# Attention with residual norms on one core: a third y tile, longer norm waits, and another split of the softmax sums

## The chip, the cores and the metric

The kernel runs on one core of one Trainium2 chip. Its five instruction streams are TensorE (PE; its weight loads, which overlap the matmuls, are shown as PEld), VectorE (DVE), ScalarE (ACT), GpSimd (POOL) and SyncE (SP), which here only issues DMAs. The metric is device time in microseconds (us), lower is better.

## What is computed

The input is x with 8 frames of 2048 rows and 256 channels, and an adjacency matrix of 2048 x 2048 that masks the attention. Cut to what matters:

```
qkv = x @ w_qkv ; split into q, k, v of 8 heads x 32
scores = q @ k.T / sqrt(32), -1e9 where adj == 0
t = softmax(scores) @ v
u = layernorm(x + t) * ln1_g + ln1_b
h = relu(u @ w1 + b1)
w = layernorm(u + h @ w2 + b2) * ln2_g + ln2_b
out = layernorm(x + w)
```

Each output row thus goes through three layer norms. Everything is in fp32.

## The kernel before

**Blocks.** The rows of a frame are cut into four chunks of 512 query rows (`qc`), the heads into two halves of four heads (`g`), the keys into 16 blocks of 128 rows (`mb`). One item is `(f, qc, g, mb)`: 128 keys against 512 queries for four heads. There are 8 x 4 x 2 x 16 = 1024 items, 128 to a frame, 32 to a chunk, 16 to a group `(f, qc, g)`. The scores are kept with the keys on the partitions, so no softmax needs a transposition, and no maximum is subtracted.

**One pass of the loop** (lines 599 to 629) is called pass t here, counted within the frame where a number below 129 is given. It issues, in this order: mask loads and new side work, then `advance(t)` (side work that is due), the exponential of item t+1 (ACT, L237, in place on one p tile of 128 x 2048), the scores of item t+2 (eight PE matmuls, L230, then two mask additions on DVE, L233, from PSUM into a new p tile), the product with V of item t (eight matmuls, L249, into one PSUM bank over the 16 blocks), and `add_up` of item t. There are 12 p tiles.

**The sums under the softmax.** The 16 exponentials of a group have to be added over the keys. That is split three ways. `POOLED` blocks are added on POOL into the tile of block 0 (L271). Blocks of a chain in `MOVED` are added by a DMA that accumulates in memory (issued by POOL, L268) into the tile of the chain's first block; each such DMA must find the one before it in its chain landed. `ALONE` is not added. `denominator` then lets TensorE sum what is left, four tiles, with a matrix of ones (L315): eight matmuls a tile into one PSUM bank. It copies the result with ACT (L317), transposes it and takes reciprocals. In the very last group the blocks from 11 on are not added beforehand, and TensorE takes eight tiles.

**Side work** is written as generators, kept in the list `fill`, sorted by a due time. Each pass gives a credit of 2200 PE cycles (`STEP`), which does not add up over passes:

```python
state["credit"] = min(max(state["credit"], 0) + STEP, KEPT)
return finish or state["credit"] >= UNIT or min(due) <= t
```

A unit of eight matmuls of 512 columns costs 2048, four transposes 1400. So a pass carries one unit or four transposes, and more than that only when something is past its due time. A generator's `yield n` sleeps n passes; `BANK` asks for the one spare PSUM bank, `MORE` keeps it for the next unit (its generator is then the holder, and nobody else gets the bank), `WAIT` keeps it while nothing may be issued yet. `TURNED` waits for the buffer of the feed-forward, `ROOM` for the number of tails in flight, `INPUTS` for a slot among three input tiles.

**A chunk's end.** Two passes after a group's last item (time `t`) its `denominator` starts, due at t + 8. When the second half's is done, `outcome` (L333) asks for `ROOM`, takes a `y` tile (two of them), transposes and scales the attention result (`divide`, DVE L353) and lets POOL issue a DMA that adds x to it (L339). `begin` is the chunk's last item + 6. At begin + 10, due at begin + 26, `tail` starts: `norm` (statistics on DVE, L278 and L279, one row of tiles per pass; four small operations on POOL, L283 to L287; two passes later four activations on ACT, L290), `feed_forward` (transposes, then POOL's L459 and L461, then w1 and w2 matmuls at L54, and DVE's L483), a second `norm`, POOL's L363 and L365, a DMA that adds x (L367), seven passes of sleep, a third `norm`, and the output's DMA on SP (L370). For the chunk before the very last, `per=2` takes two rows of tiles per pass, starting at begin + 5 with due at begin + 8. The very last chunk has its own `finish`, cut into two halves of rows that are issued alternately.

**Projections.** `NEXT` (L546) says at which pass of a frame work for the next frame begins: `turn` transposes x, `ask` computes queries, `project(c, g)` a K tile and a V tile. These come from pools of 11 buffers each (L71, L73). A K or V tile of this frame's chunk c and half 0 is last read at pass 96 + 4c + 3.

**Queues.** ACT, DVE, POOL and SP each work strictly in the order of issue. So an addition on POOL, the four small operations of a norm, the g and b rows of a tail and the issue of accumulating DMAs all stand in one line, and so do the exponentials and the activations of a norm on ACT. SP's line holds the loads of x and masks and the output.

Of the kernel before, what the change touches and what calls it, by code (L numbers as in the profile page):

```python
# [61 lines left out]
def fast_path(ctx, tc, cst, x, adj, out, RS):  # L62
# [5 lines left out]
    dp = ctx.enter_context(tc.tile_pool(name="dp", bufs=1, space=bass.MemoryType.DRAM))  # L68
    mkp = ctx.enter_context(tc.tile_pool(name="mkp", bufs=MB // 2 + 1))
    ld = ctx.enter_context(tc.tile_pool(name="ld", bufs=LD))  # L70
    kp = ctx.enter_context(tc.tile_pool(name="kp", bufs=3 * NCK - 1))  # L71
    qp = ctx.enter_context(tc.tile_pool(name="qp", bufs=4))
    vp = ctx.enter_context(tc.tile_pool(name="vp", bufs=3 * NCK - 1))  # L73
    pp = ctx.enter_context(tc.tile_pool(name="pp", bufs=12))
    work = ctx.enter_context(tc.tile_pool(name="work", bufs=1))
    yp = ctx.enter_context(tc.tile_pool(name="yp", bufs=2))
    op = ctx.enter_context(tc.tile_pool(name="op", bufs=1))
    small = ctx.enter_context(tc.tile_pool(name="small", bufs=4))

# [174 lines left out]

    POOLED = (0, 3, 6, 8, 11, 13, 15)
    MOVED = ((1, 4, 7, 10), (2, 5, 9, 12))
    ALONE = 14

    ENDED = MB - 5
    SUM = 4
# [11 lines left out]
    def norm(t, per=1):  # L274
        mv = small.tile([P, TPC, nc.vector.BN_AGGR_DIM], F32, name="mv")
        for j in range(TPC):
            st = small.tile([P, nc.vector.BN_STATS_DIM], F32, name="st")
            nc.vector.bn_stats(st, t[:, j, :])  # L278
            nc.vector.bn_aggr(mv[:, j, :], st)  # L279
            if j % per == per - 1:  # L280
                yield 1
        rs = small.tile([P, TPC], F32, name="rs")
        nc.gpsimd.tensor_scalar(rs, mv[:, :, 1], EPS, 1.0, op0=ALU.add, op1=ALU.mult)  # L283
        nc.gpsimd.tensor_tensor(rs, rs, cst["mhalf"], ALU.pow)  # L284
        nb = small.tile([P, TPC], F32, name="nb")
        nc.gpsimd.tensor_tensor(nb, mv[:, :, 0], rs, ALU.mult)
        nc.gpsimd.tensor_scalar(nb, nb, -1.0, 1.0, op0=ALU.mult, op1=ALU.mult)  # L287
        yield 2
        for j in range(TPC):
            nc.scalar.activation(t[:, j, :], t[:, j, :], AF.Identity, bias=nb[:, j:j + 1], scale=rs[:, j:j + 1])  # L290
            if j % per == per - 1:
                yield 1
# [3 lines left out]

    def denominator(f, qc, g, ready):
        grp = (f, qc, g)
        blocks = [ALONE] + [chain[0] for chain in MOVED + (POOLED,)]
        late = {len(blocks) - 1: ready}  # L300
        if (f, qc, g) == items[-1][:3]:
            blocks = [POOLED[0], 11, 12, MOVED[1][0], 13, 14, MOVED[0][0], 15]
            late = {n: len(items) - k for n, k in ((2, 2), (3, 1), (4, 1), (5, 0), (6, 0), (7, 0))}
        yield BANK
        ps = bank()
        for n, block in enumerate(blocks):
            if n:
                yield MORE
            while state["now"] < late.get(n, 0):
                yield WAIT  # L310
            term = PT.pop((f, qc, g, block))
            state["credit"] -= 4 * CH
            for h in range(4):
                r = D * h
                nc.tensor.matmul(ps[r:r + D, :], cst["ones"], term[:, h, :], start=(n == 0), stop=(n == len(blocks) - 1))  # L315
        dT = op.tile([P, CH], F32, name="dT")
        nc.scalar.copy(dT, ps)  # L317
        yield 1
        yield BANK
        ps = bank()  # L320
        transposes(ps, [dT[:, j::TPC] for j in range(TPC)])
        if g == 0:
            RC[f, qc] = op.tile([P, TPC, H], F32, name="rc")
        rc = RC[f, qc]
        den = ps.rearrange("p (j c) -> p j c", c=P)[:, :, ::D]
        nc.vector.reciprocal(rc[:, :, 4 * g:4 * g + 4], den)
        nc.vector.tensor_tensor(RS[:, 0], RS[:, 0], den, ALU.add)
        nc.vector.tensor_tensor(RS[:, 1], RS[:, 1], den, ALU.min)
        if g == 1:
            begin = items.index((f, qc, g, LAST)) + SUM + 2  # L330
            start(begin, outcome(f, qc) if (f, qc) != (F - 1, NCK - 1) else finish(f, qc), begin)

    def outcome(f, qc):  # L333
        yield ROOM
        state["tails"] += 1
        xin = x[f, qc * CH:(qc + 1) * CH, :].rearrange("(p j) c -> p j c", p=P)
        y = yp.tile([P, TPC, C], F32, name="y")
        yield from divide(f, qc, y)
        nc.gpsimd.dma_start(y, xin, accum_op=ALU.add)  # L339
        begin = items.index((f, qc, 1, LAST)) + SUM + 2  # L340
        if (f, qc) == (F - 1, NCK - 2):
            start(begin + 5, tail(f, qc, y, xin, 2), begin + 8)
        else:
            start(begin + 10, tail(f, qc, y, xin), begin + 26)

    def divide(f, qc, y):
        rc = RC.pop((f, qc))
# [9 lines left out]
    def tail(f, qc, y, xin, per=1):  # L357
        yield from norm(y, per)
        yield from feed_forward(y)
        yield 1  # L360
        z = y
        yield from norm(z, per)
        nc.gpsimd.tensor_tensor(z, z, rows(cst["g2r"]), ALU.mult)  # L363
        yield 1
        nc.gpsimd.tensor_tensor(z, z, rows(cst["be2r"]), ALU.add)  # L365
        yield 1
        nc.gpsimd.dma_start(z, xin, accum_op=ALU.add)  # L367
        yield 7
        yield from norm(z, per)
        nc.sync.dma_start(out[f, qc * CH:(qc + 1) * CH, :].rearrange("(p j) c -> p j c", p=P), z)  # L370
        state["tails"] -= 1
# [65 lines left out]
    def finish(f, qc):  # L437
        y = yp.tile([P, TPC, C], F32, name="y")
        xr, xb = state["rows"]
        yield from divide(f, qc, y)  # L440
        yT, hT = (work.tile([P, 2, CH], F32, name=n) for n in ("turned", "hT"))
        dst = out[f, qc * CH:(qc + 1) * CH, :].rearrange("(p j) c -> p j c", p=P)
        both = [half_rows(h, y, xr, xb, yT, hT, dst) for h in range(2)]
        while both:
            for e in list(both):
                if next(e, both) is both:
                    both.remove(e)

    def feed_forward(y):
        yield TURNED  # L450
# [18 lines left out]
                columns(ps, w1s[:, a, d * P:(d + 1) * P], yT[:, a, :], start=(a == 0), stop=(a == 1))  # L469
            nc.scalar.activation(hT[:, d, :], ps, AF.Relu, bias=cst["b1s"][:, d:d + 1], scale=1.0)  # L470
        state["turned"] = False
        yield 1
        z = y
        for jj in range(0, TPC, 2):
            yield BANK
# [28 lines left out]
    def advance(t, finish=False):  # L504
# [15 lines left out]
        for e in list(fill):  # L520
            while e[2] is not None and e[0] <= t and e is not state["holder"]:
# [4 lines left out]
                elif e[2] < INPUTS:  # L526
                    inputs = inputs and not any(u is not None for u in live[:INPUTS - e[2]])
                    if not inputs:
                        break
                elif e[2] == TURNED and state["turned"] or e[2] == ROOM and state["tails"] == 2:  # L530
                    break
                resume(e, t)
            while e is state["holder"] and more():
# [7 lines left out]
    def ask(f, c):  # L541
# [2 lines left out]
        give(xT)  # L544

    NEXT = {1: [(turn, 0)], 2: [(ask, 1)], 20: [(turn, 1)], 34: [(ask, 2)], 40: [(project, 0, 0)], 50: [(turn, 2)],  # L546
            60: [(project, 1, 0)], 66: [(ask, 3)], 72: [(turn, 3)], 80: [(project, 2, 0)], 98: [(ask, 0)], 100: [(project, 3, 0)],
            104: [(project, 0, 1)], 108: [(project, 1, 1)], 112: [(project, 2, 1)], 116: [(project, 3, 1)]}

    def begin():  # L550
        todo = deque((qc, c) for qc in range(NCK) for c in range(NCK))
# [319 lines left out]
```

## Time and profile before

| what | us |
|---|---|
| time, median of 3 runs (lowest to highest) | 3245.36 (3242.5 to 3246.28) |
| the profiled execution's own time | 3246.02 |
| its span, first to last instruction | 3244.1 |
| PE busy, 28996 matmuls | 3109.4 (96%) |
| DVE busy | 2735.7 (84%) |
| POOL busy | 2592.2 (80%) |
| ACT busy | 2435.8 (75%) |
| L271, sums on POOL, 381 times | 4.793 each |
| L268, issue of an accumulating DMA on POOL, 383 times | 0.956 each |
| L233, mask addition on DVE, 2048 times | 1.218 each |
| L363, L365, L459, L461 on POOL, 31 times each | 2.663, 2.687, 2.552, 2.679 each |
| L339, L367, issue of the DMAs that add x, 31 times each | 0.960, 1.071 each |
| L283, L284, L286, L287 on POOL, 93 times each | 0.194, 1.036, 0.201, 0.195 each |
| mean granted TensorE clock | 0.985 of full speed |

The profile is of one execution. A line of the timeline gives start, duration, engine, line of the kernel, operation, what is written from what, and in brackets the idle time of the engine before it with what ended it; "issue" there is a time in which the profile shows nothing that was waited for. The chain of waits is followed back from the last instruction: each piece is what the next one waited for. Matmuls are pipelined and their ends are modelled, so that a busy PE is not always a PE at its peak. Times are counted from the span's start.

### The profile page before, as it was taken

Reading aid. Unit: us, or ns where it says so; the run is one execution under the profiler, and the core shown is the slowest. Engines: PE = TensorE matmul, PEld = TensorE weight load, DVE = VectorE, ACT = ScalarE, POOL = GpSimd, SP = SyncE. Lnnn points to the kernel's source line nnn. Section 1 sums busy time; section 2 is a strip of 40 time slices with the busy share of each in tenths; the row PEclk is TensorE's granted clock in tenths of the full one; section 3 lists DMA queues with packets and bytes.
Section 4 is the critical chain, followed back from the end, with each engine's and each line's share of the span. In section 5 each row is a group of like instructions: output and inputs, shape, how many; then the busy total and the mean of one; then the engine's idle time right before and its main releaser. Section 6 shows DMA issues by size and latency. Waiting matters only on the chain.

```text
span 3244.1 us, 68406 instructions
## 1 busy us (share of the span) xinstructions
PE 3109.4 (96%) x28996; PEld 979.0 (30%) x28996; DVE 2735.7 (84%) x3203; ACT 2435.8 (75%) x1941; POOL 2592.2 (80%) x1358
## 2 busy tenths in 40 slices
PE   7899999999999999999999999999999999998985
PEld 4222333223332233322233323323233323332222
DVE  4888888888888888888988888888888888888975
ACT  3667778777777777778777778777778777777774
POOL 0568888888878888788887888888888788878884
PEclk8899999999999999999999999999999999999998
DMA  9688779778879788788787879878788878877763
GB/s 320 145 181 185 183 176 199 178 177 196 181 176 207 171 188 193 159 195 200 178 181 174 185 174 221 177 167 198 173 192 197 177 168 198 181 171 161 166 145 86
DMA packets 153240, 590.52 MB, mean 182 GB/s; under 512 B 15040, under 2 KB 67776, under 8 KB 103904
## 3 DMA queue, kind: packets, MB, share of 16 engines
q0 software_dynamic: 64416, 434.80, 66.9%
q1 hardware_dynamic: 87696, 149.98, 13.1%
q8 instruction: 229, 3.75, 0.4%
q10 hardware_dynamic: 816, 1.31, 0.1%
q14 instruction: 83, 0.68, 0.1%
HBM read 146.67 MB, written 37.75 MB: 57 GB/s over the span
## 4 chain that ended last, share of the span: by engine, by line
PE 75%; DVE 7%; POOL 5%; issue 4%; DMA 4%; ACT 2%; DVEq 0%; POOLq 0%; ACTq 0%
PE s L230 27%; PE x L249 24%; PE x L54 14%; PE x L315 6%; DVE p L233 6%; PE x L95 4%; DMA p<-p 3%; POOL p L271 2%; ACT p L237 1%; DMA mask<-md 1%; POOL y L365 1%; DVE st L278 1%; POOL y L363 0%; POOL y L461 0%; POOL y L459 0%
## 5 line engine op out<-in xcount | busy, mean ns | idle before, releaser
L233 DVE TENSOR_TENSOR p<-s,mask 128x1024 f32<-128x1024 f32 x2048 | 2409.3, 1218 | 372.7 <-PE s L230 209.9
L237 ACT ACTIVATE p<-p 128x2048 f32<-128x2048 f32 x1024 | 1956.1, 1910 | 521.4 <-DVE p L233 465.6
L271 POOL TENSOR_TENSOR p<-p 128x2048 f32<-128x2048 f32 x381 | 1825.5, 4793 | 223.7 <-ACT p L237 221.3
L230 PE MATMUL s<-qT,kT 32*128 32x512 f32 x8192 | 1173.8, 643 | 40.8 <-DVE p L233 35.9
L249 PE MATMUL x<-p,v 128*32 128x512 f32 x8192 | 1096.0, 607 | 16.7 <-ACT p L237 16.4
L268 POOL DMA_DIRECT2D p<-p x383 | 359.3, 956 | 306.9 <-ACT p L237 88.3
L230 PEld LDWEIGHTS s<-qT,kT 32*128 32x128 f32 x8192 | 321.1, 183 | 644.7 <-DVE p L233 587.2
L249 PEld LDWEIGHTS x<-p,v 128*32 128x32 f32 x8192 | 161.6, 108 | 797.8 <-issue 310.6
L315 PE MATMUL x<-p,ones 128*32 128x512 f32 x2080 | 268.2, 594 | 17.9 <-POOL p L271 11.1
L290 ACT ACTIVATE y<-y,nb,rs 128x256 f32<-128x256 f32 x372 | 218.7, 590 | 40.4 <-POOL nb L287 40.4
L54 PE MATMUL x<-in,wqkv 128*32 128x512 f32 x1888 | 243.5, 592 | 0.0
L278 DVE BATCH_NORM_STATS2 st<-y 128x6 f32<-128x256 f32 x372 | 154.9, 416 | 5.1 <-DMA y<-in_x_dram 5.1
L54 PE MATMUL x<-turned,w1s 128*32 128x512 f32 x992 | 123.5, 596 | 0.4 <-ACT in L166 0.4
L54 PE MATMUL x<-w2s,hT 128*32 128x256 f32 x2016 | 121.8, 382 | 2.1 <-DVE y L483 2.1
L54 PEld LDWEIGHTS x<-wqkv,in 128*32 128x32 f32 x3584 | 102.2, 110 | 63.4 <-issue 58.9
L315 PEld LDWEIGHTS x<-p,ones 128*32 128x32 f32 x2080 | 66.3, 110 | 178.2 <-issue 140.4
L54 PE MATMUL x<-wqkv,in 128*32 128x128 f32 x3584 | 117.3, 273 | 0.0
L54 PEld LDWEIGHTS x<-in,wqkv 128*32 128x32 f32 x1888 | 61.7, 110 | 140.9 <-issue 113.7
L284 POOL TENSOR_TENSOR rs<-rs,mhalf 128x4 f32<-128x4 f32 x93 | 96.3, 1036 | 7.8
L54 PEld LDWEIGHTS x<-w2s,hT 128*32 128x32 f32 x2016 | 65.4, 111 | 75.0 <-issue 33.0
L363 POOL TENSOR_TENSOR y<-y,g2r 128x1024 f32<-128x1024 f32 x31 | 82.5, 2663 | 5.3 <-ACT y L290 5.3
L461 POOL TENSOR_TENSOR y<-y,be1b2r 128x1024 f32<-128x1024 f32 x31 | 83.0, 2679 | 0.6
(116 smaller groups left out, 1335.7 us busy)
## 6 DMA issues: line engine op xcount, KB each, us to landing
p<-p POOLq DMA_DIRECT2D x383, 1024.0 KB, 10.4
in<-xd SPq DMA_DIRECT2D x87, 512.0 KB, 10.6
mask<-md SPq DMA_DIRECT2D x248, 128.0 KB, 7.9
y<-in_x_dram POOLq DMA_DIRECT2D x62, 512.0 KB, 8.1
p<-in_adj_dram SPq DMA_DIRECT2D x16, 1024.0 KB, 10.7
out_dram<-y SPq DMA_DIRECT2D x31, 512.0 KB, 6.2
in<-in_x_dram SPq DMA_DIRECT2D x29, 512.0 KB, 15.5
xd<-in SPq DMA_DIRECT2D x28, 512.0 KB, 11.2
```

The lines of the kernel that those rows point to most:

```text
L54: nc.tensor.matmul(out[r:r + D], lhsT[:, r:r + D], rhs, start=start, stop=stop)
L95: nc.tensor.transpose(ps[:, j * P:(j + 1) * P], s, ident)
L230: nc.tensor.matmul(ps2[half][:, j, :], KT[f, mb // TPC, g][r:r + D, (mb % TPC) * P:(mb % TPC + 1) * P], QT[f, qc, g][r:r + D, :], start=Tr ...
L233: nc.vector.tensor_tensor(pt[:, 2 * half:2 * half + 2, :], ps, MK[f, qc, mb // 2][:, mb % 2, None, :].to_broadcast([P, 2, CH]), ALU.add)
L237: nc.scalar.activation(PT[item], PT[item], AF.Exp, scale=1.0 / math.sqrt(D))
L249: nc.tensor.matmul(O[grp][r:r + D, :], V[f, mb // TPC, g][:, mb % TPC, r:r + D], PT[item][:, h, :], start=(mb == 0), stop=(mb == LAST))
L268: nc.gpsimd.dma_start(PT[f, qc, g, chain[0]], PT.pop(item), accum_op=ALU.add)
L271: nc.gpsimd.tensor_tensor(first, first, PT.pop(item), ALU.add)
L278: nc.vector.bn_stats(st, t[:, j, :])
L284: nc.gpsimd.tensor_tensor(rs, rs, cst["mhalf"], ALU.pow)
L290: nc.scalar.activation(t[:, j, :], t[:, j, :], AF.Identity, bias=nb[:, j:j + 1], scale=rs[:, j:j + 1])
L315: nc.tensor.matmul(ps[r:r + D, :], cst["ones"], term[:, h, :], start=(n == 0), stop=(n == len(blocks) - 1))
```

## The change

The change takes one buffer from each of the pools of K and V tiles and gives one to the pool of y tiles; `ROOM` then admits three tails. The blocks are split anew among POOL (now 0, 3, 6, 8, 10, 12, 14), the DMA chains (1, 4, 7, 11 and 2, 5, 9, 13) and TensorE alone (15), and the four tiles reach TensorE in another order. The sleeps of a tail are longer: four passes instead of two between a norm's POOL part and its ACT part (three where per=2), three instead of one before w2, nine instead of seven before the third norm (eight where per=2). A tail starts at begin + 11, due at begin + 28. In the last frame all tails take two rows per pass and start at begin + 9, due at begin + 12. `finish` sleeps one pass after each round of its two halves. Some projections begin later in the frame, as their buffers come free later.

```diff
-    kp = ctx.enter_context(tc.tile_pool(name="kp", bufs=3 * NCK - 1))
+    kp = ctx.enter_context(tc.tile_pool(name="kp", bufs=3 * NCK - 2))
-    vp = ctx.enter_context(tc.tile_pool(name="vp", bufs=3 * NCK - 1))
+    vp = ctx.enter_context(tc.tile_pool(name="vp", bufs=3 * NCK - 2))
-    yp = ctx.enter_context(tc.tile_pool(name="yp", bufs=2))
+    yp = ctx.enter_context(tc.tile_pool(name="yp", bufs=3))
...
-    POOLED = (0, 3, 6, 8, 11, 13, 15)
-    MOVED = ((1, 4, 7, 10), (2, 5, 9, 12))
-    ALONE = 14
+    POOLED = (0, 3, 6, 8, 10, 12, 14)
+    MOVED = ((1, 4, 7, 11), (2, 5, 9, 13))
+    ALONE = 15
...
@@ norm
-        yield 2
+        yield max(5 - per, 2)
@@ denominator
-        blocks = [ALONE] + [chain[0] for chain in MOVED + (POOLED,)]
-        late = {len(blocks) - 1: ready}
+        blocks = [ALONE, MOVED[0][0], POOLED[0], MOVED[1][0]]
+        late = {2: ready - 1, 3: ready}
         if (f, qc, g) == items[-1][:3]:
-            blocks = [POOLED[0], 11, 12, MOVED[1][0], 13, 14, MOVED[0][0], 15]
+            blocks = [POOLED[0], 11, 12, MOVED[0][0], 13, 14, MOVED[1][0], 15]
@@ outcome
-        if (f, qc) == (F - 1, NCK - 2):
-            start(begin + 5, tail(f, qc, y, xin, 2), begin + 8)
+        if f == F - 1:
+            start(begin + 9, tail(f, qc, y, xin, 2), begin + 12)
         else:
-            start(begin + 10, tail(f, qc, y, xin), begin + 26)
+            start(begin + 11, tail(f, qc, y, xin), begin + 28)
@@ tail
-        yield 7
+        yield 10 - per
@@ finish
         while both:
             for e in list(both):
                 if next(e, both) is both:
                     both.remove(e)
+            yield 1
@@ feed_forward
-        yield 1
+        yield 3
         z = y
@@ advance
-                elif e[2] == TURNED and state["turned"] or e[2] == ROOM and state["tails"] == 2:
+                elif e[2] == TURNED and state["turned"] or e[2] == ROOM and state["tails"] == 3:
@@ NEXT
-            60: [(project, 1, 0)], 66: [(ask, 3)], 72: [(turn, 3)], 80: [(project, 2, 0)], 98: [(ask, 0)], 100: [(project, 3, 0)],
-            104: [(project, 0, 1)], 108: [(project, 1, 1)], 112: [(project, 2, 1)], 116: [(project, 3, 1)]}
+            60: [(project, 1, 0)], 66: [(ask, 3)], 72: [(turn, 3)], 98: [(ask, 0)], 100: [(project, 2, 0)],
+            104: [(project, 3, 0)], 108: [(project, 0, 1)], 112: [(project, 1, 1)], 116: [(project, 2, 1)], 120: [(project, 3, 1)]}
```

## The prediction

> **What bounds the kernel now.** I read the busy times first: PE is busy 96% of the span, so little can be won unless that busy time hides waiting. The windows of 100 us show where PE is not full.
>
> ```profile
> 800.00:900.00 100.00, 100.00 (x964) 31.15 (x960) 88.16 (x102) 78.81 (x61) 87.83 (x47) 1.00 0.87 194
> ...
> 1000.00:1100.00 100.00, 97.47 (x911) 30.76 (x911) 88.49 (x106) 79.05 (x64) 81.22 (x44) 1.00 0.86 196
> ...
> 3100.00:3200.00 100.00, 86.64 (x705) 24.14 (x704) 77.29 (x99) 67.14 (x53) 77.99 (x47) 0.97 0.65 134
> ```
>
> (Columns: busy us and count of PE, PEld, DVE, ACT, POOL; clock; DMA share; GB/s.) Some windows are full, some lose 2 to 4 us, at clock 1.00. To size the losses I took from the timeline the distance between the first L249 matmuls of successive passes. They fall on few values: 2.92 us with one unit of side work (8 matmuls of L315 or L54), 3.78 with two, 2.65 to 2.75 with four transposes, 2.49 to 2.56 with none. So a unit costs 3.78 - 2.92 = 0.86, the block alone 2.92 - 0.86 = 2.06, and a pass with no side work loses about 0.48, because DVE's two mask additions (2 x 1.218) set it. Heavy passes lose nothing.
>
> Against those values the excess in frames 1 to 6 sums to 36.3 us, nearly at the same passes of each frame: 11.9 at passes 63-64, 17.6 at 83-85, 2.9 at 97, 3.9 elsewhere. Frame 0 has 6.7 at 35-36; frame 7 has 6.5 at 63-64 and 8.2 at 107-108. POOL and ACT of frame 2 show the cause of 63:
>
> ```profile
> 1025.65 4.58 POOL L271 TENSOR_TENSOR p<-p 128x2048 f32<-128x2048 f32 x1
> 1030.20 0.89 POOL L268 DMA_DIRECT2D p<-p  x1
> 1038.16 0.86 POOL L268 DMA_DIRECT2D p<-p  x1 [7.08 <-issue]
> 1038.72 4.89 POOL L271 TENSOR_TENSOR p<-p 128x2048 f32<-128x2048 f32 x1
> ...
> 1045.38 0.20 POOL L287 TENSOR_SCALAR nb<-nb 128x4 f32<-128x4 f32 x1
> ```
>
> ```profile
> 1045.61 0.60 ACT L290 ACTIVATE y<-y,nb,rs 128x256 f32<-128x256 f32 x1 [3.48 <-POOL nb L287]
> ```
>
> The DMA sum of block 10 adds into the tile into which block 7's sum, issued at 1024.74, has not landed; POOL stands 7.08 us behind it, the sum of block 11 and the norm's four small operations queue up, ACT waits for nb two passes after it was issued, and the exponential behind that is late for PE. At 83-85 it is the sum of block 15:
>
> ```profile
> 1095.70 2.68 POOL y L363
> 1098.44 4.13 issue
> 1102.57 2.67 POOL y L365
> 1106.41 4.58 POOL p L271
> 1112.10 1.90 PE s L230 x8
> ```
>
> Before 1095.10 POOL had idled 5.32 us before the DMA of block 12 (9's not landed), then the tail's L363, L365 and L367 lay between the sums; PE waited 2.00 us for block 15's (ended 1111.0). How long such a DMA takes is in the view of tile p:
>
> ```profile
> DMA to landing us min/median/max: 6.8/10.4/17.5
> ```
>
> Three passes are 8.8 us, less than the median landing.
>
> **The change, part by part.** Counts stay: six L271 and six L268 a group, four blocks of L315, the same tails and projections; the pools trade one K and one V tile for a y tile. What moves is order.
>
> **Sums.** Chains 1,4,7,10 and 2,5,9,12 become 1,4,7,11 and 2,5,9,13: the last steps are four passes (11.7 us) apart, with L271s between. Pooled sums go at 8,10,12,14. Per pair POOL needs 4.79 + 0.96 = 5.75 of 5.84 us: no slack from 8 to 14, so what enters late stays late. Taking exponentials 2.92 us apart, block n's ending at 2.92n, a quiet group runs: sum 8 from 23.6 to 28.4, DMA 9, sum 10 from 29.4, DMA 11, sum 12 from 35.2, DMA 13 issued about 40.9, sum 14 from 41.8 to 46.6. The POOLED chain thus ends a pass sooner than with 15, and block 15 goes from ACT straight to TensorE.
>
> **When PE needs them.** In frame 2 PE reached the fourth L315 block at 1111.0 - 2.0 = 1109.0; block 15's exponential had ended at 1095.2. So the fourth block is needed 13.8 us after exponential 15 in the groups whose denominators start at once (two a frame: passes 49 and 81), 19.6 after exponential 13; the third 13.8 after exponential 14. Elsewhere they run one to six passes later. `ready - 1` and `ready` only hold the planner's bank that long; they are no waits of an engine. The price is here: MOVED[1] becomes the fourth block and its last DMA comes a pass later. In an early group (tail operations: one norm, 1.6; L339, 0.96; a second norm before 13) I get DMA 13 issued at exponential 13 + 6.3, landing at 16.7 by the median, against 19.6: 2.9 us of room. At the longest landing it is 23.8, late by 4.2. I take no wait mostly and 1 us now and then: 7 us over frames 1 to 6. On POOL, sum 14 and the tail queue behind DMA 13's wait for 9's landing (issued at 28.4, landed by 39: hidden by sum 12, as long as it takes under 11.6). Block 13's tile also comes free a pass later than 12's; DVE waited 3.8 us for such tiles in the whole run, so I cost that at nothing.
>
> **Longer waits.** In before, a norm's ACT part comes two passes after its POOL part; ACT waits 3.48 us where POOL is 7 to 11 us behind. Four passes are 11.7 us: the 40.4 us of L290's waiting for nb should nearly go. Start + 11, two more passes per norm, yield 3 and 9 lengthen a tail by 11 passes, 60 to some 71 (outcome to output), so three overlap at a period of 32: the third y tile and ROOM 3 are then needed and never block. On POOL it moves L363, L365, L367 from positions 11 to 15 of a group to about 5 to 7, and L459, L461 to 14 to 16. The worst group then takes, from sum 3 on: norm 1.6, DMA 4, L363 2.66, DMA 5, L365 2.69, sum 6, L367 1.07; sum 8 is 5.6 us late and stays so, DMA 13 is issued 8.5 after its exponential and lands at 18.9, in a group whose denominators start a pass later (needed at 22.5). Two us of L483's wait for L461 at 97 have two more passes. So of the 36.3 I let 29 go (the 7 above stay). What is late next is PE itself.
>
> A sentence on a page: the Trainium skill, "DMA: Bandwidth & Descriptors", section "Anatomy of one DMA — SWDGE (gpsimd) path", gives about 2.0 us plus bytes at 436 GB/s, an estimate of 4.4 us for these 1 MB. By it no sum three passes behind would wait, the spacing would be worth nothing, and without the 17.6 us of passes 83-85 the forecast would be some 3229. The trace has 6.8 as its shortest landing, so the measurement decides.
>
> **Projections** start later (80 to 100 and so on) because a K tile is free only then. In before (2,0) ran at passes 106-109 all the same, since its input slot and a tail came first. Shifted tails leave, as I order it by due times, empty passes at 48, 62 and 94 in place of 48 and 80: one more, 0.48 x 6 = 3 us. Bounds: none, or four more a frame, 12.
>
> **Frame 0.** At pass 35 PE waits for block 12's DMA, issued at 180.4 behind block 9's and landing in 15.0. Now the third block is the POOLED sum (done about 186) and block 13's DMA, issued about 180.5, is the fourth, needed 3 us later: 5 of 6.7 us go.
>
> **Frame 7.** At 107 DVE waits for L339's landing:
>
> ```profile
> 3118.78 9.49 DMA y<-in_x_dram
> 3128.36 0.44 DVE st L278
> ```
>
> The norm was issued five passes after begin; nine passes are four times 2.5 us later: all 8.2 go. At 63-64 a tail of frame 6 and one with per=2 now put L363, L365, L459, L461 together at positions 6 to 8; I get the last DMA some 3 us late: 3.5 of 6.5 go. All tails take two rows a pass: two statistics add up to 0.9 us per norm to a DVE-bound pass, six more norms so, 0 to 6, I take 5. Sum: -7.
>
> **End.** Finish now yields after each round. The last tail is some eight passes later, so its L363 and L365 (2.4 each here) come between finish's POOL operations, and its last norm still follows finish's on DVE, as now:
>
> ```profile
> 3233.54 0.42 DVE L278 BATCH_NORM_STATS2 st<-y 128x6 f32<-128x256 f32 x1
> ...
> 3239.90 0.33 SPq L370 DMA_DIRECT2D out_dram<-y  x1
> ```
>
> Finish's second half waits for L380 behind L365: +1 (bounds: -5, if the norm slips ahead of finish, and +5). Block 10 of the last group, now summed on POOL, has its exponential at 3181.2; with 4.8 us it is there before TensorE's first L315 at 3191.3: nothing.
>
> **Sum**: -29 + 3 - 5 - 7 + 1 = -37, from the profiled execution's 3246.0: 3209. The median shown is 0.7 lower. I move up by 3, since any new pile-up adds: **3212**.
>
> **Rivals.**
> - Half the gain: the pile-ups move with the tails rather than go (a denser 8 to 14 never catches up). For: no slack there. Against: POOL works 86.5 us of a chunk's 95.7. Half of the 36.3, frames 0 and 7 as above, empty passes 4: -18 - 12 + 4 + 1 = -25; new waits of 0.4 us in the four late groups of each frame give back 24 x 0.4 = 10: -15, 3231. Chance 0.2.
> - No change: the tails' waiting passes and empty passes give back what the sums win; 12 empty, 10 waits, DVE at two rows 6, two thirds of the stalls kept: about 3243. Chance 0.08.
> - Slower: block 13's DMA. If landings are 15 us or more once DMAs 11 and 13 run beside loads, each denominator waits for it. It breaks even at 37/62 = 0.6 us per group; with the longest landing, 17.5, 4.2 us in 16 early groups and 0.9 in 46 others are 67 + 41 = 108, against 37 + 7 won: 3246 + 64 = 3310 at worst, at half the waits 3256. Against: last links landed in 8.2 to 12.7 in most groups. Chance 0.12.
>
> My forecast has 0.6. A measurement tells 0.2%, 6.5 us, from no change. Faster 0.8, same 0.08, slower 0.12. All stalls gone without cost would be 3246 - 58 = 3188; the range that leaves 2 in 10 out is 3192 to 3243.
>
> **What would show it.** Right: L268's idle "until issue" and "DMA p<-p" (80.9 and 75.5) falls below half; L290's wait for nb goes below 10; no L315 waits for L271; frames are 383 to 386 apart. Wrong: L315 waits for DMA p<-p in most groups, or many passes of 2.5 us without side work.

## The result and the profile after

The changed kernel takes 3330.46 us (median of four runs, 3324.94 to 3335.74) against 3243.93 before (3240.75 to 3246.28): a ratio of 1.0267, 95% interval 1.0247 to 1.0287. The forecast was 3212 us, faster; the result is 86.5 us above the kernel before. The profiled execution took 3328.53 us, its span is 3326.8. The work is the same, and PE is less full:

```profile
PE 3128.9 (94%) x28996; PEld 981.0 (29%) x28996; DVE 2739.6 (82%) x3203; ACT 2438.5 (73%) x1941; POOL 2602.9 (78%) x1358
```

The same windows of 100 us as shown of before (busy us and count of PE, PEld, DVE, ACT, POOL; clock; DMA share; GB/s):

```profile
800.00:900.00 100.00, 99.27 (x984) 31.37 (x976) 85.60 (x101) 78.04 (x62) 82.52 (x44) 1.00 0.80 176
...
1000.00:1100.00 100.00, 91.39 (x792) 27.43 (x788) 79.15 (x95) 71.29 (x57) 76.69 (x41) 0.95 0.78 177
...
3100.00:3200.00 100.00, 90.42 (x736) 24.85 (x736) 84.51 (x99) 74.21 (x58) 82.36 (x44) 0.98 0.76 161
```

From 1000 to 1100 there are 792 matmuls where there were 911, and the clock is no longer 1.00. Counted from the exponentials that open them, frames 1 to 5 last 400.7 to 403.4 us (384.1 to 390.1 before), frame 6 394.4 (391.0), frame 7 397.6 (397.1), and what follows the last exponential 52.8 (48.1).

**What was meant to go went.** The groups of L290 and L315 (count, busy us, mean ns, idle time before and what ended it):

```profile
L315 PE MATMUL x<-p,ones 128*32 128x512 f32 x2080 | 266.9, 594 | 14.8 <-DMA p<-p 14.8
L290 ACT ACTIVATE y<-y,nb,rs 128x256 f32<-128x256 f32 x372 | 217.7, 591 | 3.0 <-POOL nb L287 3.0
```

ACT waits 3.0 us for nb where it waited 40.4, and no L315 waits for POOL's L271 any more (11.1 us before). POOL's L268 stands 31.5 us for DMA p<-p (75.5 before) and 53.0 for "issue" (80.9). Three other things came, told below.

The end has the order it had, the last norm's statistics on DVE and 6.4 us later the output's DMA:

```profile
3316.23 0.42 DVE L278 BATCH_NORM_STATS2 st<-y 128x6 f32<-128x256 f32 x1
...
3322.60 0.33 SPq L370 DMA_DIRECT2D out_dram<-y  x1
```

**First, PE waits for a load.** PE's timeline in frame 2, near pass 62:

```profile
1059.79 0.66 PE L95 MATMUL x<-ident,y 128*128 128x128 f32 x4
1060.38 1.14 PE L230 MATMUL s<-qT,kT 32*128 32x512 f32 x8
1061.45 1.07 PE L249 MATMUL x<-p,v 128*32 128x512 f32 x8
1069.54 1.09 PE L95 MATMUL x<-ident,in 128*128 128x128 f32 x4 [7.03 <-DMA in<-in_x_dram]
1070.56 2.09 PE L230 MATMUL s<-qT,kT 32*128 32x512 f32 x8
1072.58 1.94 PE L249 MATMUL x<-p,v 128*32 128x512 f32 x8
```

The chain of waits from 1055 to 1075 has the load in one piece:

```profile
1044.59 24.82 DMA in<-in_x_dram
1069.40 0.14 issue
1069.54 1.09 PE x L95 x4
```

This is `turn(2)`, the transposition of the next frame's x for chunk 2. Both kernels issue its load at pass 55. Before, the transposition came at passes 74 and 75 and the landing (19 to 26 us) was hidden; now it stands at pass 62, since nothing else was ready there. PE reaches it 17.9 us after the issue (1069.54 - 7.03 - 1044.59), and that is all the cover a landing of 24.8 us has. And behind the wait PE is slow: eight L230 take 2.09 us, 1.14 elsewhere.

**Second, DVE has two jobs in one pass.** The chain from 990 to 1010, passes 41 to 43 of frame 2:

```profile
1001.37 2.27 DVE p L233 x2
1003.63 0.34 DVE st L278
1003.97 0.02 issue
1004.00 0.07 DVE mv L279
1004.06 0.03 issue
1004.10 0.66 DVE y L353
1004.76 2.26 DVE p L233 x2
```

From one pair of mask additions to the next are 3.39 us: the pair itself, a tail's second-norm statistics and the divide of the next chunk. A pass of four transposes takes 2.65 to 2.75 otherwise. It happens twice in each chunk.

**Third, p tiles come free late** at passes 93 to 101. The waits of after (engine, tile, line, what for: us in all, times, longest):

```profile
PE x L95 <- DMA in<-in_x_dram: 36.1, 6, 7.1
DVE p L233 <- DMA p<-p: 28.0, 22, 2.7
```

Before the change the first line is not there, and the second was 1.7 us (together with the waits for POOL's sums 3.8, against 29.5 now).

### The profile page after: what moved, and what is told of

It is laid out like the page before. It is cut to its first block, busy times and chain, and to the rows that moved or that the text cites. A ratio compares the mean times of both kernels' runs of the same rounds, so it can differ in the third digit from the quotient of the medians.

```text
span 3326.8 us, 68503 instructions
## 1 busy us (share of the span) xinstructions
PE 3128.9 (94%) x28996; PEld 981.0 (29%) x28996; DVE 2739.6 (82%) x3203; ACT 2438.5 (73%) x1941; POOL 2602.9 (78%) x1358
## 4 chain that ended last, share of the span: by engine, by line
PE 61%; DVE 14%; DMA 13%; POOL 4%; issue 3%; ACT 2%; SPq 0%; DVEq 0%; POOLq 0%; ACTq 0%
PE s L230 23%; PE x L249 19%; PE x L54 13%; DVE p L233 11%; DMA p<-p 9%; PE x L315 5%; DMA in<-in_x_dram 4%; POOL p L271 2%; PE x L95 2%; ACT p L237 2%; DVE st L278 1%; DVE y L353 1%; POOL y L363 0%; DMA mask<-md 0%; DVE mv L279 0%
## 5 line engine op out<-in xcount | busy, mean ns | idle before, releaser
L233 DVE TENSOR_TENSOR p<-s,mask 128x1024 f32<-128x1024 f32 x2048 | 2410.3, 1219 | 469.9 <-PE s L230 306.3
L271 POOL TENSOR_TENSOR p<-p 128x2048 f32<-128x2048 f32 x382 | 1865.7, 4884 | 282.0 <-ACT p L237 281.8
L230 PE MATMUL s<-qT,kT 32*128 32x512 f32 x8192 | 1176.9, 644 | 77.6 <-DVE p L233 72.6
L268 POOL DMA_DIRECT2D p<-p x382 | 392.7, 1046 | 194.6 <-ACT p L237 71.9
L230 PEld LDWEIGHTS s<-qT,kT 32*128 32x128 f32 x8192 | 321.7, 184 | 689.0 <-DVE p L233 642.2
L315 PE MATMUL x<-p,ones 128*32 128x512 f32 x2080 | 266.9, 594 | 14.8 <-DMA p<-p 14.8
L290 ACT ACTIVATE y<-y,nb,rs 128x256 f32<-128x256 f32 x372 | 217.7, 591 | 3.0 <-POOL nb L287 3.0
L363 POOL TENSOR_TENSOR y<-y,g2r 128x1024 f32<-128x1024 f32 x31 | 74.4, 2399 | 74.5 <-ACT y L290 74.5
L315 PEld LDWEIGHTS x<-p,ones 128*32 128x32 f32 x2080 | 66.4, 110 | 175.8 <-issue 141.0
L460 POOL TENSOR_TENSOR y<-y,g1r 128x1024 f32<-128x1024 f32 x31 | 83.2, 2682 | 0.0
```

Source lines behind the costliest of these rows:

```text
L230: nc.tensor.matmul(ps2[half][:, j, :], KT[f, mb // TPC, g][r:r + D, (mb % TPC) * P:(mb % TPC + 1) * P], QT[f, qc, g][r:r + D, :], start=Tr ...
L233: nc.vector.tensor_tensor(pt[:, 2 * half:2 * half + 2, :], ps, MK[f, qc, mb // 2][:, mb % 2, None, :].to_broadcast([P, 2, CH]), ALU.add)
L268: nc.gpsimd.dma_start(PT[f, qc, g, chain[0]], PT.pop(item), accum_op=ALU.add)
L271: nc.gpsimd.tensor_tensor(first, first, PT.pop(item), ALU.add)
L460: nc.gpsimd.tensor_tensor(y, y, rows(cst["g1r"]), ALU.mult)
```

## The experiments

Eighteen kernels were run. Ratios are against the kernel before, run on the same chip. "The sums" are the new `POOLED`, `MOVED`, `ALONE` and the order of the blocks in `denominator`; "the tails" are all the rest of the change.

### Which half costs

The sums alone, in the kernel before:

```diff
-    MOVED = ((1, 4, 7, 10), (2, 5, 9, 12))
+    MOVED = ((1, 4, 7, 11), (2, 5, 9, 13))
...
-        late = {len(blocks) - 1: ready}
+        late = {2: ready - 1, 3: ready}
```

> The kernel before, with only the split of the sums and the order of TensorE's four blocks changed. T: POOL's waits for landings before blocks 10 and 12 go, no new pass order: 3219 to 3238 us against 3244 of before. R: most of the 86 us of loss, 3290 to 3330.

Measured 3198.1 us, ratio 0.9871 (0.9854 to 0.9887). Better than expected. POOL is hardly ever late, and PE's L315 waits 0.7 us for landings in the whole run:

```profile
L268 POOL DMA_DIRECT2D p<-p x382 | 408.2, 1070 | 74.8 <-ACT p L237 46.0 <-issue 23.0 <-ACT dT L317 2.3
L290 ACT ACTIVATE y<-y,nb,rs 128x256 f32<-128x256 f32 x372 | 218.4, 589 | 3.0 <-POOL nb L287 3.0
```

The tails alone (the changed kernel with the three constants and the order of the blocks as before):

> The changed kernel with the split of the sums and the order of TensorE's four blocks as before the change; all else of the change stays. T: the wait for the x load (42 us) and the meetings on DVE (30) stay, the late sums at 95 to 101 (up to 25) may go, and POOL's waits for landings come back: 3305 to 3335 us. R: the whole loss goes, 3235 to 3250.

Measured 3389.59, ratio 1.0457 (1.044 to 1.0474): beyond both numbers. The rival, that the new sums cost, is out. The tails cost, 149 us here. Later, with two of the costs found below taken out of the tails (sleep ahead of w2 of one pass, `yield 12 if c == 2 else 5` in `turn`), the old sums were tried again:

> The changed kernel with the feed-forward's sleep of one pass and the later load for chunk 2 (3225.7 us when run so), but with the sums of the kernel before. Theory that the new sums are what frees GpSimd of the waits for the landings: the waits return, 3245 to 3285 us. Rival, that the longer norm waits and the third row tile relieve GpSimd by themselves: at most 3243 us.

Measured 3310.13, ratio 1.0206 (1.0183 to 1.023), more than expected; with the new sums the same tails take 3225.65. The waits for landings are back (L268 170.2 us for DMA p<-p, 59.4 with the new sums), ACT's for nb are not (17.0). So the sums are worth 43 us in the kernel before (3240.73 on that chip, 3198.1), 59 in the changed one and 84 here.

### The wait for the load, and the sleep ahead of w2

The load gets more time:

```diff
@@ turn
-        yield 5
+        yield 12 if c == 2 else 5
```

> The changed kernel, with one edit: the x load for chunk 2 of the next frame may land for 12 passes instead of 5 before its transposition is put into PE's line. Theory T (the new time is in PE's line: in passes 62 of frames 1 to 5 the planner finds nothing else and takes that transposition, whose load has not landed; 8.3 us each, 42 in all; the rest is statistics that meet the scaling of the attention result on DVE, some 5 us a frame, and late sums at passes 95 to 101, some 4 a frame): 42 less, 3 back for an empty pass 62, and up to 18 back if the stall had covered the late sums of the group that ends at pass 63: 3290 to 3308 us against 3330. Rival R (the new split of the sums costs it all, block 13's DMA being last): no change, 3325 to 3335.

Measured 3284.3, ratio 1.0134 (1.0117 to 1.0151). The wait is gone and 46 us with it, a little more than the 22 to 40 expected.

The sleep between w1 and w2 as it was:

```diff
@@ feed_forward
-        yield 3
+        yield 1
         z = y
```

> The changed kernel with one edit: the feed-forward sleeps one pass before w2, as before, instead of three. The order of issue then has w2 ahead of the group's denominators, so that the second norm's statistics come three passes sooner, ahead of the scaling of the attention result, and the denominators two passes later. T: the meetings on DVE (5 us a frame) mostly go, and so do the late sums at 95 to 101 (4 a frame), the wait at 62 stays: 3330 - 30 to 50, 3280 to 3300 us. R: only the later denominators help: 3305 to 3330.

Measured 3246.9, ratio 1.0025 (1.0008 to 1.0041): 84 us, where 30 to 50 were expected. The ten runs of this kernel lie between 3238.62 and 3262.69, further apart than those of any other here, so the 84 is good only to some ten us. Both together:

> Both edits of the two runs before in the changed kernel: one pass of sleep before w2, and 12 passes for chunk 2's x load. T: the edits add up but for what the first already took of the wait at pass 62 (4.0 us a frame left in five frames): 3247 - 20 to 30, 3215 to 3228 us; frames 383 to 386 us apart. R, in its form after those runs (the new split of the sums pays only with the old tails, since the longer tails crowd POOL and the DMAs): the wait shows up elsewhere, 3235 to 3250, and L315 or the mask additions wait for DMA sums.

Measured 3225.65, ratio 0.9951 (0.9938 to 0.9965), as expected. That the sleep costs was now the theory, and the test was to add it to the good version with the sums alone (`yield 1` to `yield 3`, nothing else):

> The kernel before with the new sums (3198.1 us) and one more edit: three passes of sleep instead of one ahead of the feed-forward's second products. Theory that the sleep itself costs (the denominators go ahead of the second products on the bank, and the second norm's statistics land beside the divide on VectorE): 3223 to 3243 us. Rival, that the sleep is harmless without the later tails and the third row tile: within 5 us of 3198.

Measured 3323.0, ratio 1.0252 (1.0231 to 1.0273): 125 us for two passes of sleep. The direction was right, the size far off, so something beyond the meeting on DVE is in it. I had two candidates: the order on PE (w2 now comes behind the denominators) and the places of the second norm.

### The second norm three passes later

This edit tells them apart, since it leaves PE's order as it is, matmul by matmul:

```diff
@@ tail
         yield from feed_forward(y)
-        yield 1
+        yield 4
         z = y
         yield from norm(z, per)
```

In the changed kernel with the later load:

> The changed kernel with the later load for chunk 2 (3284.3 us when run without this edit), and three further passes of sleep between the feed-forward and the second norm, so that the norm's statistics no longer meet the divide on VectorE while TensorE's order stays. If the meeting on VectorE is what the feed-forward's sleep costs (5.1 us in each frame, and what follows from it): 3245 to 3260 us. If it is the denominators that come two passes earlier: 3275 to 3290.

Measured 3210.38, ratio 0.9903 (0.9884 to 0.9922): 74 us less, where the theory of the meeting had 25 to 40. In the changed kernel itself, as the only edit:

> The changed kernel (3330.5 us) with one edit: the second norm three passes later. In the kernel with the later load for chunk 2 the same edit took away 74 us. If the two stalls add: 3250 to 3262 us. If the later norm also hides the wait for chunk 2's load: 3205 to 3225. If it only works with the later load: above 3290.

Measured 3210.88, ratio 0.9898 (0.9881 to 0.9916). This was the second of the three cases expected. One number in one line takes 120 us away, with PE's order unchanged and `turn(2)` still at pass 62, though PE no longer waits there; the kernel is then at the time that was forecast. So in the changed kernel it is the place of the second norm, with what follows it in the tail, that costs, and not the order on PE by itself. The timeline of DVE where the divide of chunk 0 is, in frame 3:

```profile
1363.79 0.68 DVE L353 TENSOR_TENSOR y<-x,rc 128x512 f32<-128x512 f32 x1
1364.38 2.34 DVE L233 TENSOR_TENSOR p<-s,mask 128x1024 f32<-128x1024 f32 x2
1366.65 0.68 DVE L353 TENSOR_TENSOR y<-x,rc 128x512 f32<-128x512 f32 x1
1367.24 2.34 DVE L233 TENSOR_TENSOR p<-s,mask 128x1024 f32<-128x1024 f32 x2
1369.51 0.41 DVE L278 BATCH_NORM_STATS2 st<-y 128x6 f32<-128x256 f32 x1
```

Divide and statistics no longer share a pass: 2.86 us from pair to pair. And the load lands sooner. The DMAs issued in the 35 us around the load (KB each, median us to landing), with the later norm:

```profile
p<-p POOLq DMA_DIRECT2D x5, 1024.0 KB, 12.6
mask<-md SPq DMA_DIRECT2D x5, 128.0 KB, 15.5
...
in<-in_x_dram SPq DMA_DIRECT2D x1, 512.0 KB, 16.2
```

and of the changed kernel, 45 us around the same load of frame 3:

```profile
p<-p POOLq DMA_DIRECT2D x6, 1024.0 KB, 12.2
mask<-md SPq DMA_DIRECT2D x5, 128.0 KB, 24.3
...
in<-in_x_dram SPq DMA_DIRECT2D x1, 512.0 KB, 24.7
```

Over frames 1 to 6 the load takes 10.3 to 17.4 us with the later norm and 18.8 to 24.9 without. What lies nearest to it on POOL, in frame 3 of the changed kernel (the load is issued at 1447.73):

```profile
1445.36 2.69 POOL L365 TENSOR_TENSOR y<-y,be2r 128x1024 f32<-128x1024 f32 x1
1447.67 1.23 POOL L268 DMA_DIRECT2D p<-p  x1
1448.35 1.46 POOL L367 DMA_DIRECT2D y<-in_x_dram  x1
```

A sum's DMA goes out 0.06 us ahead of the load, and the DMA that adds x to y 0.6 us behind. I took the latter for the cause and moved it alone (the sleep ahead of it from one pass to four):

> The changed kernel (3330.5 us) with the tail's residual DMA (L367, x added into the tile) three passes later and the second norm where it is; TensorE's order is unchanged. In the changed kernel the DMA was issued 0.6 us behind chunk 2's load of x, which then took 24.7 us; with the later second norm it came four passes behind, and the load took 16.2. If this DMA delays the load: no wait for the load in frames 1 to 5, the statistics still beside the divide, 3280 to 3292 us. If the second norm's place is what matters: above 3315.

Measured 3308.26, ratio 1.0192 (1.0174 to 1.021). Between the two, and the trace says no: the load still takes 19.6 to 25.9 us and PE waits for it up to 8.1, though this DMA is now 10.4 us away; where the 22 us that this run gained came from stays open. The opposite edit, the later norm without the two sleeps of one pass on either side of L365, so that this DMA comes 6.1 us behind the load:

> The changed kernel with the second norm three passes later (3210.9 us) and without the two passes of sleep between GpSimd's two tail operations and the residual DMA, so that this DMA is again queued one pass after where the changed kernel has it. If the DMA delays chunk 2's load of x: the wait for it is back at 3 to 7 us in most frames, 3230 to 3255 us. If the later second norm alone does it: 3208 to 3215.

Measured 3223.35, ratio 0.9933 (0.9915 to 0.9951): the load takes 10.2 to 12.1, less still, and PE never waits for it; the 12 us lie in pass 63, where PE waits some 1 us a frame for DVE, in the late denominators and in the last frame. (L365 is the DMA's line in this kernel.) So the nearness of L367 is not the cause.

The accumulating DMA of the sums was the next suspect. Where one is issued in the same 0.1 us as the load (the changed kernel, the run with the later load alone, the run with L367 later), the load takes 22 to 26 us in 16 of 18 cases; in the versions at 3210.38, 3210.88 and 3223.35, where the next one comes 3 us behind or later, it takes 10.2 to 17.5. In the changed kernel L363 and L365 stand in POOL's line among the sums just there; with the later norm they come behind, and two sums' DMAs go out 5.4 and 4.8 us before the load. But other runs break the pattern: with the tails alone four loads took 24.3 to 25.5 us though the next such DMA came 3.8 to 4.1 us behind, and in the run at 3323 five took 17.3 to 20.7 with the next one 4.3 to 5.9 us behind. So why the load lands sooner with the later norm is not shown. No run moved a sum's DMA alone.

In the kernel with the sums alone and the sleep of three passes (3323.0), the same edit, its last sleep one pass shorter for want of a third y tile:

> The kernel before with the new sums and the feed-forward's sleep of three passes (3323.0 us when run so), and with the second norm three passes later (its last wait is one pass shorter, 6 in place of 7). TensorE's order is that of the run at 3323, the denominators still ahead of the second products. If the sleep costs because the second norm's statistics meet the divide on VectorE, and the norm's GpSimd part then falls among late sums: 3205 to 3240 us. If it costs because the denominators go first: above 3290.

Measured 3413.67, ratio 1.0526 (1.0507 to 1.0544). The time lies where the theory of PE's order had it (above 3290), but neither theory explains it: PE's order is that of the run at 3323, and the statistics have left the divide, yet it is 91 us slower. ACT's timeline and POOL's show where it is lost:

```profile
1310.03 0.60 ACT L290 ACTIVATE y<-y,nb,rs 128x256 f32<-128x256 f32 x1 [8.80 <-POOL nb L287]
```

```profile
1295.46 4.87 POOL L271 TENSOR_TENSOR p<-p 128x2048 f32<-128x2048 f32 x1
1300.01 2.64 POOL L461 TENSOR_TENSOR y<-y,be1b2r 128x1024 f32<-128x1024 f32 x1
1302.32 1.16 POOL L268 DMA_DIRECT2D p<-p  x1
1302.92 5.11 POOL L271 TENSOR_TENSOR p<-p 128x2048 f32<-128x2048 f32 x1
1308.12 0.19 POOL L283 TENSOR_SCALAR rs<-mv 128x4 f32<-128x4 f32 x1
```

A norm's small operations stand on POOL behind L461 of a tail and two late sums, though its statistics were done at 1293, and ACT stands 8.80 us before the exponential that PE needs; L290 waits 177.4 us for nb in the whole run. At 3323 it is the same at passes 66 and 67 (77.5 in all). Set pass by pass against the run with the sums alone, the run at 3323 takes 123 us more, 54 of them at passes 66 and 67 and some 26 where statistics meet the divide. The run at 3413.67 wins back 26 at pass 66 and some 21 at the meetings, but loses 47 at pass 2, 49 at pass 98 and 23 at pass 72 (over all frames); at the first two ACT stands 60 and 70 us for nb. So a tail's place is what counts, not how long it sleeps. Whether the longer norm waits are what makes the later norm good in one kernel and bad in the other was the last run (a norm's ACT part two passes after its POOL part again, and two passes of sleep behind the norm, in the version at 3210.88):

```diff
@@ norm
-        yield max(5 - per, 2)
+        yield 2
...
+        yield 3 - per
```

> The changed kernel with the second norm three passes later (3210.9 us), and with each norm's ScalarE part two passes after its GpSimd part again, as in the kernel before; two passes of sleep behind the norm keep all later steps in their passes. TensorE's order is unchanged. If the longer norm waits carry part of the gain: ScalarE waits for nb again (40.4 us in all in the kernel before), 3225 to 3255 us. If the new sums alone keep GpSimd punctual: within 4 us of 3211.

Measured 3214.6, ratio 0.9913 (0.9896 to 0.9929): within 4, and the wait for nb is only 11.7 us. No: where POOL is punctual the longer waits buy next to nothing. What is left between the two kernels is the start of the tails (begin + 11 against + 10), the third y tile with its later projections, and the last frame; these were not separated, and why the same edit helps in one and hurts in the other stays open beyond what POOL's line shows.

### The last frame and the end

In the version at 3225.65, only the tail of the last chunk but one takes two rows per pass; the last frame's other tails go as in the earlier frames:

```diff
@@ outcome
-        if f == F - 1:
+        if (f, qc) == (F - 1, NCK - 2):
             start(begin + 9, tail(f, qc, y, xin, 2), begin + 12)
```

> The run with both edits, and in the last frame only the last tail takes two rows per pass and starts at begin + 9; the other two go as in the frames before. T: in frame 7 two statistics in a pass make DVE the bound for up to 1 us, 3 to 4 us a tail pair: 3 to 10 us less than with both edits alone. If two rows per pass cost nothing: within 2 us of it.

Measured 3212.81, ratio 0.9911 (0.9897 to 0.9924): 13 us, more than expected; frame 7 goes from 397.9 to 385.3. The same edit in the version at 3210.38:

> The changed kernel with the later load for chunk 2 and the later second norm (3210.4 us when run so), and with the last frame's first tails as the kernel before has them, so that only the last tail but for the others takes two rows in a pass. The same edit took 13 us from another version (3225.7 to 3212.8). If the two rows in a pass cost by themselves: 3196 to 3202 us. If they cost only where the statistics met the divide: 3206 to 3211.

Measured 3207.42, ratio 0.9892 (0.9874 to 0.991): 3 us. So these tails (two rows per pass and the earlier start; the edit takes back both) cost mostly where POOL and DVE were already late. `finish` without its new sleep, in the version at 3225.65 (its `yield 1` taken out):

> The run with both edits, and finish issues all its rounds at once as before, without a sleep after each. The stretch from the last exponential to the end was 48.1 us before the change and 52.8 with it, and in it PE waited 8.8 in place of 5.2 us for finish's first activations. If the tail's operations that now come between finish's rounds cost that: 3 to 5 us less than with both edits alone, nothing changed up to the last exponential. If it is the later tail itself: no difference.

Measured 3228.53, ratio 0.9959 (0.9946 to 0.9973): 3 us more, against expectation; the end is 51.4 in place of 49.7. The sleep helps. The sums alone with the last tail at begin + 9:

> The kernel before with the new split of the sums (3198 us), and the last tail started at begin + 9, due at begin + 12, as the change has it. DVE's wait for the DMA that adds x at pass 107 of frame 7 (6.5 us of PE's time, 8.2 with what follows) goes: 3188 to 3194 us, if the end stays as it is; the tail is four passes later, so up to 5 us may come back at the end: 3190 to 3199.

Measured 3195.27, ratio 0.9857 (0.9842 to 0.9872), as expected: frame 7 is 7.1 us shorter, the end 3.8 longer. With the sleep in `finish` too:

> The kernel before with the new sums and the last tail's start and due pass three passes later (3195.3 us when run without this edit), and with the sleep of one pass put back into each round of the finish. If the last tail's third norm and the finish's rounds then share the end, as the run without the finish's sleep suggested (1.7 us at the end), 3190 to 3194 us. If the sleep only helped the longer tails, 3195 to 3197.

Measured 3193.52, ratio 0.985 (0.983 to 0.987). It is the fastest version found, 137 us ahead of the changed kernel; the last step alone is within the spread.

## Why the prediction was wrong

Set pass by pass against the version that differs in the one number (3210.88), the changed kernel's passes take 113 us more. 49 are at passes 59 to 65 (the wait for the load and the slow PE behind it, 46 of it in frames 1 to 5), 35 at the passes where statistics meet the divide (5.1 in each of frames 1 to 6), 21 at 92 to 102 (p tiles and denominators late), 8 elsewhere.

- **Longer waits: this step failed.** It followed the lengthened tail on POOL only ("On POOL it moves L363, L365, L367 …") and took everything that is later for harmless because it is later. The second norm's statistics were not placed on DVE at all in frames 1 to 6; two more passes of sleep put them beside the divide of the next chunk, 35 us that the sum had at nothing. POOL's own places were worked out too kindly as well: the sums came so late in some groups that L233 waited 28.0 us for DMAs on p tiles (29.5 with those for POOL's sums), which the step on block 13's tile had "at nothing" from the 3.8 of before.
- **Projections** failed with it: "empty passes at 48, 62 and 94" priced an empty pass 62 at 0.48 us. It is not empty. The planner fills it with `turn(2)`, and the load behind that takes longer than the 17.9 us it has: with the slow PE after it, 8.2 to 9.9 us a frame in frames 1 to 5 (46 in all), in place of 0.48. Passes 48 and 94 are empty as said, and 79 and 91 with them. I had ordered the side work by its due times without asking, for what moves forward, whether its input is there.
- **Sums**: right, and undersized. 29 were to go from frames 1 to 6 and 5 from frame 0; alone they give 43. In the two traces frames 1 to 6 are 35.5 shorter, close to the whole 36.3, frame 0 is 6.8 and frame 7 6.7 shorter. The 7 held back for block 13's DMA were not needed there (L315 waits 0.7 us for landings).
- **The page weighed**, the Trainium skill, "DMA: Bandwidth & Descriptors", section "Anatomy of one DMA — SWDGE (gpsimd) path", with 4.4 us as an estimate for such a DMA: the view of L268 of the changed kernel has none so short, and the new split of the sums, spacing included, was worth 43 us, so the measurement was the right side.

```profile
DMA to landing us min/median/max: 6.9/10.8/16.1
```

- **L290's wait for nb**: right in the changed kernel (3.0, "below 10"), but the longer waits were not needed for it: the sums alone bring it to 3.0, the tails alone to 5.9, and without the longer waits it is 11.7 in the version at 3210.88.
- **Frame 0, frame 7, the end**: in the version at 3210.88 frame 0 is 5.7 shorter (5 said), frame 7 9.7 shorter (7 said), the end 3.3 longer (1 said), frames 1 to 6 together 20.8 shorter (26 said). The gain of passes 107 and 108 is 8.3 where 8.2 was said, in the changed kernel too. In the changed kernel itself frame 7 gained nothing, since its other passes took it back (10.4 us more than in the version at 3210.88, 2.5 of it where statistics meet the divide); "I take 5" for two rows per pass was, together with the earlier start, 3 where things are punctual and 13 where they are not.
- **The rivals**: slower had 0.12, by block 13's DMA. That is not what happened: L315 waits 14.8 us for landings in the whole run; that is more than the 6.9 of before, but with the waits for POOL (11.1 before, none now) less than the 17.9 in all. Block 13's DMA landed in 10.3 us at the median and 14.9 at the longest. "The pile-ups move with the tails" came nearest in kind; it was priced at half the gain, and with nothing on DVE or on the loads.
- **The signs**: nb, L271 and L268's wait for DMA p<-p came out as the right path had them, L268's "issue" did not fall to half (80.9 to 53.0), and frames 1 to 5 are 401 to 403 us apart in place of 383 to 386. Of the signs of the wrong path, L315 waited for landings 13 times, not in most of the 64 groups; the signs watched the sums and empty passes, and the loss lay elsewhere.

The version at 3210.88 comes near the sum (−34 of span, 3244.1 to 3210.1, where −37 was said), but that is in part luck. The sums alone take 51 us off the span of these traces (3244.1 to 3193.3), so the rest of the change still costs 17 there: a gain taken too small and a cost not foreseen nearly cancel. Nor does it make the forecast right, for the kernel that was to be forecast had these places in its code to be read.

## What to carry to other kernels

When a chain of side work is shifted in a periodic schedule, write down for each in-order engine, the vector engine included, which operations then share a step, modulo the period; here two passes of sleep cost 84 us in one kernel and 125 in another, and three more passes for the next step took 120 away in the first and added 91 in the second. For whatever moves forward into the gap, compare the time since its load was issued with the longest landing seen, not with the median. Add one part at a time: here one part alone was worth 1.3%, and the other hid it.

## What the hardware showed that was not expected

A long wait costs PE more than itself. Around the wait of 7.03 us above (columns as in the windows before; the clock is the third number from the end):

```profile
1062.00:1066.00 4.00, 0.51 (x8) 0.00 (x0) 2.01 (x2) 1.34 (x1) 1.17 (x2) 0.92 1.03 221
1066.00:1069.50 3.50, 0.00 (x0) 0.00 (x0) 0.00 (x0) 0.00 (x0) 3.50 (x2) 0.50 0.96 213
1069.50:1072.00 2.50, 2.46 (x12) 1.24 (x12) 0.00 (x0) 1.34 (x2) 2.50 (x3) 0.50 1.08 370
1072.00:1074.00 2.00, 2.00 (x12) 0.40 (x12) 1.23 (x2) 1.06 (x1) 2.00 (x2) 0.50 1.05 228
1074.00:1076.00 2.00, 2.00 (x16) 0.30 (x8) 1.64 (x3) 0.79 (x1) 2.00 (x2) 0.60 1.03 220
1076.00:1078.00 2.00, 2.00 (x20) 0.62 (x24) 0.82 (x1) 1.12 (x1) 2.00 (x1) 1.00 1.11 231
```

The granted clock falls to 0.50 during the wait and stays there for some 6 us after it: the four groups behind the wait take 6.8 us (1.09, 2.09, 1.94, 1.68) where 3.9 is usual (0.66, 1.14, 1.07, 1.04), so that a wait of 7.03 us makes frame 2's passes there 9.9 us longer. The kernel before has it too, behind the wait of 2.00 us for block 15's sum on POOL that ended at 1111.0; over 100 us the mean hid it:

```profile
1108.00:1112.00 4.00, 2.00 (x20) 0.28 (x16) 2.36 (x2) 1.57 (x1) 3.83 (x3) 1.00 0.66 132
1112.00:1116.00 4.00, 4.00 (x22) 0.86 (x19) 1.88 (x2) 2.88 (x3) 3.83 (x4) 0.57 0.05 13
```

It does not follow every wait: in the kernel before, of the windows of 100 us between 300 and 2900 only those at 1100 and 2600 are below 1.00 (0.98 each), though PE lost time at passes 83 to 85 in every frame from 1 to 6. A long wait of PE is thus to be priced with the slow microseconds that can stand behind it. The second surprise: the landing of one and the same 512 KB load ranged from 7.8 to 25.9 us over the kernels, with the DMA engines' share near 1.0 in the windows above: a landing time read from one profile is a property of that schedule.
